# Attention with mixture-of-experts on one core: small vector work and clearing DMAs spread over the tiles of a row, and the last row's routing cut six to two

## The chip, the cores and the metric

The kernel runs on one core of a Trainium2 chip. The metric is the device time of one execution in microseconds (us), the median of three runs. The engines are named as in the profile: PE (TensorE, matrix products), DVE (VectorE), ACT (ScalarE), POOL (GpSimd) and SP (SyncE, which here only issues DMAs).

## What is computed

The input x has 8 rows of 1024 tokens with 128 features. The reference is, cut to what matters:

```python
x = x + attention(layernorm(x))       # 16 heads of 8, query l sees keys l-63 to l
x = x + moe(layernorm(x))             # 8192 tokens

# attention: softmax(q k / sqrt(8) over the 64 keys of the window) v, then Wo
# moe:
scores = softmax(xf @ w_router)       # 8 experts
expert_weights, top_experts = top_k(scores, 2)
order = argsort(flat_e, stable=True)  # tokens of an expert in order
slot = where(offsets < 2048, expert * 2048 + offsets, none)
xb = zeros(8 * 2048 + 1, 128).at[slot].set(xf[src])   # gather tokens by expert
h = gelu(xb @ w1); y = h @ w2         # per expert, 128 -> 512 -> 128
out = zeros(T, 128).at[src].add(weight * y) + bias
```

The slot of a token needs the count of all tokens ahead of it that chose the same expert, so routing goes through the rows in order.

## The kernel before

**Two phases.** Phase one does the attention, the router and the filling of `xb`, the buffer of tokens by expert in the chip's large memory. Phase two runs the experts over `xb`. The change touches phase one alone.

**Tiles.** Phase one is a loop over 64 tiles of 128 queries, 8 tiles for each of the 8 rows (L1163 to L1209; tile j of row b is called (b, j) below). Each turn of the loop does, in this order:

- `scores` of the tile two ahead: 32 small products per unit on PE (L557), then DVE takes the maximum over the keys (`mx`, L565) and prepares it in three 16-bit parts (L573). PE transposes `mx` (L582) and ACT copies it to `mxt` (L584).
- `attend` of the tile one behind: probabilities times values (`av`, L647), copied by ACT to `sums` (L655).
- if a group of tiles is complete, a `Context`: SP DMAs move the softmax denominators (`den`, L676) and the weighted values (`ctx`, L678) from `sums` into the feature layout. A group of four goes by another way, with one reciprocal on DVE (L688) between two rounds of DMAs (L673, L683, L690, L694). Later DVE divides (`scale`, L704 and L705).
- `probs` of the tile itself: the scores again in the transposed layout with the maximum taken off (`t`, L602, L619, L626), and ACT's exp (L632). The score buffers in PSUM are three, shared by `scores` and `probs`.

**Planned steps.** Between these go steps of the neighbouring rows, from a list `plan` written by hand. `at(b, j, ...)` puts a step to tile (b, j). In tile i the steps up to the second one that uses PE are issued at once, the rest (`behind`) in the next tile after `scores`. `pairs` holds ACT work that follows the context (exp of the router at L823, the `apply` of the second norm at L415), and `late` the division steps. The steps are:

- `first(b, ...)`: the attention's norm of row b. `stats` (DVE), `root` (an inverse square root by three Newton steps, L384 to L396, 13 instructions on DVE, more if part of it is on GpSimd), `rooted` (L403, L421), and `apply` (L410) for four tiles at a time, on DVE. `FOUR[0]` and `FOUR[1]` are the two halves of a row.
- `turn`, `queries`, `keys`, `values`, `spread`: the transposes and projections of the next row. `spread` sends `qt` and `kt` in block form to `qbd` and `kbd` by eight SP DMAs (L496, L499). `values` ends with two SP DMAs (L485, L487).
- `of(b, 0, ...)`: the routing of the row before. `out` (L781 to L787) is the output projection and residual, then `stats`, `root`, `softmax`, `choose` (top two, L831 to L849), `count` (PE, L858), `place` (running count, L870 to L879), `slots` (slot numbers, L887 to L890) and `keep` (adds the bias, L809, and stores the residual, L810).

`slots` also appends one scatter per token tile and choice to a queue; `put` (L903) takes them from it, as indirect DMAs issued by GpSimd, two per tile and three from row 5 on.

**Order on the engines.** The orders on PE, DVE, ACT and GpSimd are as written by hand. SP's is left to the scheduler. All engines work in order.

**Clears.** `clears()` zeroes `xb` by 16 SP DMAs of 528 KB (L315), each from a small zero tile `zeros` of four rows that is read over and over. The loop asks for one a tile from tile 1 (two from tile 14), but nothing makes the DMA wait, and the scheduler issues them all between 19 and 50 us.

**The last rows.** Row 6's routing is cut in two halves of four tiles, so that it can run inside row 7. Row 7's is done by `piece`: two pieces of four tiles, advanced by `go(piece, n)`, which does the next n of its steps. Some of these stand in the plan, the rest behind the loop, where no tiles hide them. There `put` sends out what is queued, and GpSimd sets a mark (`memset`, L1229) behind which PE does `stay_awake(38)`: 76 products of no use (L169), which keep PE's clock up until `xb` is complete.

Of the kernel before, what the change touches and what calls it, by code (L numbers as in the profile page):

```python
# [10 lines left out]
F32 = mybir.dt.float32  # L11
# [8 lines left out]
P = 128  # L20
# [4 lines left out]
E = 8  # L25
TOP_K = 2
FFN = 512
W = D + 4
# [14 lines left out]
def bc_mid(ap, n):  # L43

    return ap.unsqueeze(1).to_broadcast([ap.shape[0], n, ap.shape[1]])
# [3 lines left out]
def kernel(  # L49
# [13 lines left out]
    nc = tc.nc  # L63
    B, L, _ = x.shape
    NJ = L // P
# [4 lines left out]
    NS = CAP // P  # L70
# [21 lines left out]
    def after(ins, of):  # L92

        tc.add_manual_dep(
            ins, of.name,
            mybir.DependencyInfo(mybir.DependencyClass.Sync, mybir.DependencyReason.DATA),
            reason="a transfer in step with the tiles",
        )
# [17 lines left out]
    with ExitStack() as ph:  # L116
        c1 = ph.enter_context(tc.tile_pool(name="c1", bufs=1))
# [34 lines left out]
        for r in range(4):  # L152
            nc.sync.dma_start(
                out=wo_sb[r::4, 0:D],
                in_=wo.rearrange("(g r d) c -> r g d c", g=NQ, r=4)[r],
            )
        nc.sync.dma_start(
            out=bias_sb, in_=bias.rearrange("a b d -> (a b) d").to_broadcast([P, D])
# [33 lines left out]
        for t in (mt_32, mtf_32):  # L192
# [9 lines left out]
            out=i32s, in_=ident.rearrange("p (g q) -> p q g", g=4), axis=AX.X, op=ALU.add  # L202
# [45 lines left out]
        def permute():  # L248
# [15 lines left out]
        rev = c1.tile([P, E], F32, tag="rev", name="rev")  # L264
        limit = c1.tile([P, E], F32, tag="limit", name="limit")
        tok = c1.tile([P, NT], F32, tag="tok", name="tok")
        zeros = c1.tile([P, 4, W], F32, tag="zeros", name="zeros")

        go_on = {
            n: c1.tile([P, E * n], F32, tag=f"goon{n}", name=f"go_on{n}") for n in (2, 4, 8)  # L270
        }
        taken = [c1.tile([P, E], F32, tag=f"taken{i}", name=f"taken{i}") for i in range(2)]

# [36 lines left out]
        def clears():  # L310

            half = CAP // 2
            for i in range(2 * E):
                to = xb[i * half : (i + 1) * half, :].rearrange("(p n) d -> p (n d)", p=P)
                nc.sync.dma_start(  # L315
                    out=to.rearrange("p (m k) -> p m k", m=NS // 8),
                    in_=bc_mid(zeros.rearrange("p n d -> p (n d)"), NS // 8),
                )
                yield


        kt_b, kbd_b, qbd_b, xnt_b, mx_b = [], [], [], [], []
# [337 lines left out]
        class Context:  # L660
# [46 lines left out]
            def steps(self):  # L707

                if self.few:
                    return ((1, self.invert), (3, self.scale))  # L710
                return (
                    (1 + t * (self.b < 6), partial(self.scale, t)) for t in range(self.n)
                )

        def attend_last(b, j, pr):
# [203 lines left out]
        def at(b, j, call, *args):  # L919
            plan[b * NJ + j].append((call, args))  # L920
# [38 lines left out]
        at(0, 4, turn, 1, 1)  # L959
        at(0, 4, first, 2, "stats")  # L960
        at(0, 4, queries, 1, 1)
        at(0, 5, keys, 1, 1)
        at(0, 5, first, 2, "root", nc.gpsimd)
        at(0, 5, values, 1, 0)
        at(0, 7, first, 2, "rooted")
        at(0, 7, first, 2, "apply", FOUR[0])
        at(0, 7, values, 1, 1)
        at(1, 0, first, 2, "apply", FOUR[1])

        for b in range(1, B):
            f = (b - 1, 0)
            if b < 7:
                at(b, 0, of, *f, "out", 0, 3)
                at(b, 0, of, *f, "out", 3, 1)
                plan[b * NJ].insert(0, (begin, (b - 1, 0, NJ)))
            at(b, 1, values, b, 2)
            if b + 1 < B:
                at(b, 1, turn, b + 1, 0)  # L980
                at(b, 2, queries, b + 1, 0)
                at(b, 3, keys, b + 1, 0)
                at(b, 3, spread, b + 1, 0)
            if b < 7:
                at(b, 2, of, *f, "stats", range(2))
                at(b, 2, of, *f, "out", 4, 2)
                at(b, 3, of, *f, "out", 6, 2)
            if b + 1 < B:
                at(b, 4, values, b + 1, 0)
                at(b, 4, turn, b + 1, 1)  # L990
                at(b, 5, queries, b + 1, 1)
                at(b, 6, keys, b + 1, 1)
                at(b, 7, values, b + 1, 1)
            if b == 7:
                continue
            if b + 2 < B:
                at(b, 1, first, b + 2, "stats")
                at(b, 6, first, b + 2, "root", nc.vector)
                at(b, 7, first, b + 2, "rooted")
                at(b, 7, first, b + 2, "apply", FOUR[0])  # L1000
                at(b + 1, 0, first, b + 2, "apply", FOUR[1])
            at(b, 3, of, *f, "stats", range(2, 4))
            at(b, 3, of, *f, "root", nc.vector)
            n = b * NJ + 4
            for t, what, *args in (
                (n, "rooted"), (n, "softmax"),
                (n + 1, "choose", 0),
                (n + 2, "choose", 1),
                (n + 4, "slots"),
                (n + 4, "keep", (0,)), (n + 5, "keep", (2,)),  # L1010
                (n + 6, "keep", (4,)), (n + 7, "keep", (6,)),
            ):
                plan[t].append((of, (*f, what, *args)))
            pairs[n].append(partial(of, *f, "exp"))
            for i in range(4):
                pairs[n + i].append(partial(of, *f, "apply", range(2 * i, 2 * i + 2)))
            plan[n + 3].insert(0, (of, (*f, "count")))
            plan[n + 3].append((of, (*f, "place")))


        def half(b, j0, *steps):
# [32 lines left out]
        def piece(j0, j1):  # L1054
            f = (B - 1, j0)
            n = range(j1 - j0)
            calls = (
                (begin, B - 1, j0, j1, True),
                *((of, *f, "out", i, min(2, len(n) - i)) for i in range(0, len(n), 2)),
                (of, *f, "stats"),  # L1060
                (of, *f, "root", nc.vector),
                (of, *f, "rooted"),
                (of, *f, "softmax"),
                (of, *f, "exp"),
                (of, *f, "choose", 0),
                (of, *f, "apply", n),
                (of, *f, "choose", 1),
                (of, *f, "count"),
                (of, *f, "place"),
                (of, *f, "slots"),  # L1070
                (of, *f, "keep"),
            )
            return iter(calls)
# [3 lines left out]
                done = call(*args)  # L1077
            return done

        ends = [piece(0, 4), piece(4, 8)]  # L1080
        at(7, 4, go, ends[0], 2)
        at(7, 6, go, ends[0], 3)
        at(7, 7, go, ends[0], 5)
        at(7, 7, go, ends[1], 2)

        def values_end():
            for w in range(2):
# [69 lines left out]
        tiles = [(b, j) for b in range(B) for j in range(NJ)]  # L1157
        scores(0, 1)
        mxt = turn_max(0, 0)
        clearing = clears()  # L1160
        todo, late, behind, after_context = None, defaultdict(list), [], []
        for i, (b, j) in enumerate(tiles):
            if j == 0:  # L1163
                ctxs[b] = a2.tile([P, L], F32, tag="ctx", name=f"ctx_{b}")
                spread(b, 1) if b else None
            for _ in range(min(i, 1) if i < 14 else 2):
                next(clearing, None)
            ahead = tiles[i + 1] if i + 1 < len(tiles) else None


            def scores_ahead():
                if i + 2 < len(tiles):
                    put(1, scores(*tiles[i + 2]))

            if i:
                scores_ahead()
            for call, args in behind:
                call(*args)
            if todo is not None:
                begun, _ = attend(*todo)  # L1180
                put(1 if b >= 5 else 0, begun)
                if i - 1 in together:
                    context = Context(*together[i - 1])
                    for n, step in context.steps():
                        late[i + n if i < len(tiles) - 2 else i].append(step)
                for call in after_context:
                    call()
                after_context = []
            pr, mxt, done = probs(b, j, mxt, ahead)
            if not i:  # L1190

                for call, args in plan[0]:
                    call(*args)
                plan[0] = []
                scores_ahead()
            todo = (b, j, pr)
            put(1, done)
            if 2 <= j < 6:
                load_x(b + 3, slice(2 * j - 4, 2 * j - 2), done)
            if i in (34, 42):  # L1200
                ahead_w.append(load_w(len(ahead_w), done))

            n = [n for n, step in enumerate(plan[i]) if is_product(*step)][1:2]
            n = n[0] if n else len(plan[i])
            for call, args in plan[i][:n]:
                call(*args)
            behind = plan[i][n:]
            after_context = pairs[i]
            for call in late[i]:  # L1209
                call()  # L1210
# [3 lines left out]
        put(len(puts))  # L1214


        for which, n in ((0, 2), (1, 2), (0, 2)):
            go(ends[which], n)
        put(2)
        for n in (2, 1, 2):  # L1220
# [160 lines left out]
```

## Time and profile before

| What | Time |
|---|---|
| median of three runs | 761.75 us (760.16 to 764.14) |
| the profiled execution, device time | 762.97 us |
| span of its trace | 761.2 us |
| granted PE clock, mean | 0.941 of full speed |
| start to 47 us | PE busy 37.4 us, DVE 28.7, DMA engines 66% |
| row 2 to 3 (152 to 204 us) | PE busy 45.7 us, DVE 41.0, DMA engines 35% |
| row 7 (360 to 449 us with row 6's end) | PE busy 70.5 us, DVE 70.7, DMA engines 26% |
| between loop and experts (449 to 495 us) | PE busy 13.5 us, DVE 17.5, POOL 28.5, clock 0.58 |
| experts (495 to 761 us) | PE busy 242.4 us, DVE 35.4, POOL 197.5 |

The rows are parts of one profiled execution; the columns give the busy time in each stretch, which adds up work that overlaps. The device time of that execution is 1.8 us over its span, since what lies ahead of the first and behind the last instruction is not in the trace. The busy time of an engine says how much it has to do; which wait ends last in a stage has to be read from the order of the instructions there.

### The profile page before, as it was taken

The numbers are of one execution on the slowest core, as the hardware profiler recorded it, in microseconds if no ns is written. First come the engines' busy times: TensorE is split into PE (matmuls) and PEld (weight loads), VectorE is DVE, ScalarE is ACT, GpSimd is POOL, SyncE is SP. The second block draws the span as 40 slices with busy tenths as digits, with TensorE's granted clock in tenths as the row PEclk, the third lists the DMA queues.
The fourth block names the chain that finished last, engine by engine and source line by source line (L and its number), as shares of the span: only waits on it lengthen the run. The fifth ranks groups of instructions, "written<-read, shape, count | busy, mean of one in ns | idle before, by whom it ended". The sixth has DMA issues, their size and how long they took to land.

```text
span 761.2 us, 21771 instructions
## 1 busy us (share of the span) xinstructions
PE 634.9 (83%) x8777; PEld 468.5 (62%) x8777; DVE 389.3 (51%) x1219; ACT 364.3 (48%) x637; POOL 361.9 (48%) x366
## 2 busy tenths in 40 slices
PE   8789698897987987988979641599999999999990
PEld 7445455454555544554545430589999999898990
DVE  6664577978688778788887764121111111111010
ACT  5446367566565674674664520023444444443430
POOL 7001000332432434505416447438778787787876
PEclk9999899999999999999998965699999999999996
DMA  2982313333243433333322111236456365463333
GB/s 76 325 294 77 91 58 97 97 115 116 81 123 108 130 107 112 123 96 104 111 84 86 59 45 54 78 102 109 53 106 109 43 123 93 52 119 34 36 31 31
DMA packets 78308, 74.00 MB, mean 97 GB/s; under 512 B 13907, under 2 KB 63928, under 8 KB 77312
## 3 DMA queue, kind: packets, MB, share of 16 engines
q1 hardware_dynamic: 55296, 55.59, 23.2%
q0 software_dynamic: 22528, 16.74, 15.8%
q8 instruction: 69, 1.13, 0.7%
q14 instruction: 31, 0.25, 0.1%
q10 hardware_dynamic: 384, 0.28, 0.1%
HBM read 19.14 MB, written 30.28 MB: 65 GB/s over the span
## 4 chain that ended last, share of the span: by engine, by line
PE 28%; issue 17%; DVE 14%; POOL 14%; ACT 11%; DMA 9%; SPq 6%; POOLq 0%; DVEq 0%; ACTq 0%
POOL out_dram L1310 12%; ACT pr L632 7%; PE av L647 5%; PE t L619 5%; PE yp L1300 5%; PE hp L1289 4%; DMA out_dram<-ye,dest 4%; DVE mx L565 3%; SPq L676 2%; DMA ctx<-sums 2%; ACT mxt L584 2%; SPq L678 2%; PE t L602 2%; PE po L781 2%; PE t L626 1%
## 5 line engine op out<-in xcount | busy, mean ns | idle before, releaser
L903 POOL DMA_INDIRECT xb<-xn,si x128 | 125.5, 980 | 226.4 <-PE t L626 64.5
L1310 POOL DMA_INDIRECT out_dram<-ye,dest x128 | 197.5, 1543 | 68.4 <-issue 27.4
L632 ACT ACTIVATE pr<-t 128x1024 f32<-128x1024 f32 x128 | 123.9, 1019 | 55.0 <-PE t L626 46.2
L565 DVE TENSOR_REDUCE mx<-s 128x8 f32<-128x768 f32 x128 | 116.3, 951 | 41.0 <-PE s L557 40.9
L1300 PEld LDWEIGHTS yp<-w,hT 128*128 128x128 f32 x1024 | 124.7, 193 | 9.3 <-ACT hT L1293 6.3
L1300 PE MATMUL yp<-w,hT 128*128 128x128 f32 x1024 | 126.1, 276 | 4.6 <-DVE ye L1305 3.9
L1289 PE MATMUL hp<-xts,w 128*128 128x256 f32 (+1 forms) x528 | 122.4, 375 | 0.3 <-DVE xts L1280 0.3
L1293 ACT ACTIVATE hT<-hp 128x512 f32<-128x512 f32 x128 | 76.4, 597 | 70.3 <-PE hp L1289 68.3
L1305 DVE TENSOR_TENSOR ye<-yp,gt 128x256 f32<-128x256 f32 (+1 forms) x66 | 27.1, 415 | 161.7 <-PE yp L1300 138.9
L1289 PEld LDWEIGHTS hp<-xts,w 128*128 128x128 f32 x528 | 94.1, 192 | 10.2 <-DVE xts L1280 0.6
L655 ACT COPY sums<-av 128x512 f32<-128x512 f32 x63 | 36.9, 586 | 100.6 <-PE av L647 90.7
L647 PE MATMUL av<-pr,vbd 128*32 128x128 f32 x2016 | 71.1, 282 | 7.6 <-ACT vbd L480 2.7
L619 PE MATMUL t<-qbd,kt 32*128 32x256 f32 x1024 | 74.0, 391 | 0.4 <-issue 0.3
L647 PEld LDWEIGHTS av<-pr,vbd 128*32 128x32 f32 x2016 | 53.1, 112 | 28.9 <-ACT mxt L584 9.3
L557 PE MATMUL s<-kbd,qt 32*32 32x384 f32 x2048 | 61.0, 506 | 4.5 <-DMA kbd<-kt 4.5
L1280 ACT COPY xts<-xt 128x256 f32<-128x256 f32 (+1 forms) x57 | 21.0, 369 | 88.0 <-PE xt L1278 88.0
L619 PEld LDWEIGHTS t<-qbd,kt 32*128 32x128 f32 x1024 | 51.1, 192 | 4.4 <-issue 2.3
L809 POOL TENSOR_TENSOR x<-x,bias_sb 128x256 f32<-128x256 f32 x28 | 21.3, 764 | 51.7 <-ACT xn L415 51.4
L781 PE MATMUL po<-wo_sb,ctx 128*128 128x136 f32 x128 | 25.8, 327 | 19.9 <-DVE lg L787 9.0
L781 PEld LDWEIGHTS po<-wo_sb,ctx 128*128 128x128 f32 x128 | 18.9, 207 | 37.2 <-issue 14.9
L704 DVE RECIPROCAL den<-den 128x128 f32<-128x128 f32 x39 | 36.8, 944 | 7.5 <-DMA den<-sums 7.1
L602 PE MATMUL t<-i,mt 32*128 32x256 bf16 x448 | 28.6, 280 | 13.6 <-DVE mx L565 7.4
(185 smaller groups left out, 745.8 us busy)
## 6 DMA issues: line engine op xcount, KB each, us to landing
xb<-zeros SPq DMA_DIRECT2D x16, 528.0 KB
xe<-xb SPq DMA_DIRECT2D x7, 1056.0 KB
vbd<-vbd SPq DMA_DIRECT2D x32, 192.0 KB
kbd<-kt SPq DMA_DIRECT2D x62, 72.0 KB
qbd<-qt SPq DMA_DIRECT2D x64, 64.0 KB
out_dram<-x SPq DMA_DIRECT2D x32, 128.0 KB
w<-in_L_ffn_w_dram SPq DMA_DIRECT2D x16, 256.0 KB
x<-in_L_attn_x_dram SPq DMA_DIRECT2D x22, 128.0 KB
```

The source lines that it names most:

```text
L557: done = nc.tensor.matmul(place(g, slice(32 * blk, 32 * (blk + 1))), lhsT=qt[quad(g), q0 : q0 + 32], rhs=kbd[quad(g), :, c0 + 32 * blk : c ...
L565: nc.vector.tensor_reduce(out=part_of(mx, 0)[:, 2 * u : 2 * u + 2], in_=units[u][:, :, 0 : 4 * KB].rearrange("p g (r k) -> p g r k", r=4), ...
L602: nc.tensor.matmul(to, lhsT=mt[quad(g), 0, hq, :], rhs=i32[quad(g)].rearrange("p (w r) q -> p w r q", w=2), start=hq == 0, stop=False, ski ...
L619: nc.tensor.matmul(units[g // 2][:, g % 2, w], lhsT=kt[quad(g), q0 : q0 + P], rhs=qbd[quad(g), :, c0 : c0 + 64], start=False, stop=False, ...
L632: nc.scalar.activation(pr[:, 2 * u : 2 * u + 2], units[u], AF.Exp)
L647: last = nc.tensor.matmul(av[quad(g), k, :, w], lhsT=pair_values(vbd, 2 * j + w, g, k), rhs=pr[:, g, w, 2 * k : 2 * k + 2, :], start=True, ...
L781: nc.tensor.matmul(po[:, k, :], lhsT=ctxs[self.b][:, t0 : t0 + P], rhs=wo_sb, start=True, stop=True,)
L903: ins = nc.gpsimd.indirect_dma_start(out=xb[:, :], out_offset=bass.IndirectOffsetOnAxis(ap=slot, axis=0), in_=row, in_offset=None, bounds_ ...
L1289: nc.tensor.matmul(hp[:, c], lhsT=ws[e][0][:, (c0 + c) * P : (c0 + c + 1) * P], rhs=xt, start=True, stop=True,)
L1293: nc.scalar.activation(hT[:, c0 : c0 + per], hp, AF.Gelu_apprx_tanh)
L1300: nc.tensor.matmul(yp[:, k, :], lhsT=hT[:, c, k * P : (k + 1) * P], rhs=ws[e][1][:, c, :], start=c == 0, stop=c == NC - 1,)
L1310: add = nc.gpsimd.indirect_dma_start(out=acc, out_offset=bass.IndirectOffsetOnAxis(ap=dests[e][:, n : n + 1], axis=0), in_=ye[:, k, :], in ...
```

## The change

- **Clears.** `zeros` has two rows instead of four, so that a clear reads 264 floats (1056 bytes) at a time, and twice as many such chunks. `clears` is a generator that is sent the last product of `probs` of the preceding tile, and its DMA waits for it (`after`). One clear goes with each tile from tile 1, two with tile 14.
- **First norm.** `root` and `rooted` of row b+2 stand first in tile (b, 3)'s plan (formerly in tiles 6 and 7), `apply` for the two halves in tiles 5 and 6 (formerly tile 7 and tile 0 of the next row). For row 2 the root goes from GpSimd to DVE, with the like steps in row 0; `keys(1, 1)` comes a tile later there, behind `values(1, 0)`.
- **Routing of rows 0 to 4.** `slots` and the first `keep` come a tile later.
- **Routing of row 5** (done in row 6): `choose(1)`, `count` and `place` come a tile sooner, and `slots` at the end of tile (6, 7), a tile sooner than before.
- **Context steps.** In row 7 the division steps of a group are spread over tiles as in rows 0 to 5; only in row 6 they stay together.
- **Last row.** The pieces are six and two tiles instead of four and four, with other `go` steps: two at tile 5, nine at tile 7, and three instead of two in the second turn behind the loop. `go_on`, a constant by piece width, gets the width 6.

```diff
-        zeros = c1.tile([P, 4, W], F32, tag="zeros", name="zeros")
+        zeros = c1.tile([P, 2, W], F32, tag="zeros", name="zeros")
...
-            n: c1.tile([P, E * n], F32, tag=f"goon{n}", name=f"go_on{n}") for n in (2, 4, 8)
+            n: c1.tile([P, E * n], F32, tag=f"goon{n}", name=f"go_on{n}") for n in (2, 6, 4, 8)
...
+            behind = yield
             for i in range(2 * E):
                 to = xb[i * half : (i + 1) * half, :].rearrange("(p n) d -> p (n d)", p=P)
-                nc.sync.dma_start(
-                    out=to.rearrange("p (m k) -> p m k", m=NS // 8),
-                    in_=bc_mid(zeros.rearrange("p n d -> p (n d)"), NS // 8),
-                )
-                yield
+                into = nc.sync.dma_start(
+                    out=to.rearrange("p (m k) -> p m k", m=NS // 4),
+                    in_=bc_mid(zeros.rearrange("p n d -> p (n d)"), NS // 4),
+                )
+                after(into.ins, behind.ins)
+                behind = yield
...
-                    (1 + t * (self.b < 6), partial(self.scale, t)) for t in range(self.n)
+                    (1 + t * (self.b != 6), partial(self.scale, t)) for t in range(self.n)
...
-        at(0, 5, keys, 1, 1)
-        at(0, 5, first, 2, "root", nc.gpsimd)
         at(0, 5, values, 1, 0)
-        at(0, 7, first, 2, "rooted")
-        at(0, 7, first, 2, "apply", FOUR[0])
+        at(0, 5, first, 2, "root", nc.vector)
+        at(0, 5, first, 2, "rooted")
+        at(0, 6, keys, 1, 1)
+        at(0, 6, first, 2, "apply", FOUR[0])
+        at(0, 6, first, 2, "apply", FOUR[1])
         at(0, 7, values, 1, 1)
-        at(1, 0, first, 2, "apply", FOUR[1])
...
-                at(b, 6, first, b + 2, "root", nc.vector)
-                at(b, 7, first, b + 2, "rooted")
-                at(b, 7, first, b + 2, "apply", FOUR[0])
-                at(b + 1, 0, first, b + 2, "apply", FOUR[1])
+                plan[b * NJ + 3].insert(0, (first, (b + 2, "root", nc.vector)))
+                plan[b * NJ + 3].insert(1, (first, (b + 2, "rooted")))
+                at(b, 5, first, b + 2, "apply", FOUR[0])
+                at(b, 6, first, b + 2, "apply", FOUR[1])
...
-            n = b * NJ + 4
+
+            n, soon = b * NJ + 4, b == 6
...
-                (n + 2, "choose", 1),
-                (n + 4, "slots"),
-                (n + 4, "keep", (0,)), (n + 5, "keep", (2,)),
+                (n + 2 - soon, "choose", 1),
+                (n + 5 - 2 * soon, "slots"),
+                (n + 5, "keep", (0,)), (n + 5, "keep", (2,)),
...
-            plan[n + 3].insert(0, (of, (*f, "count")))
-            plan[n + 3].append((of, (*f, "place")))
+            plan[n + 3 - soon].insert(0, (of, (*f, "count")))
+            plan[n + 3 - soon].append((of, (*f, "place")))
+            if soon:
+                step = (of, (*f, "slots"))
+                plan[n + 3].remove(step)
+                plan[n + 3].append(step)
...
-        ends = [piece(0, 4), piece(4, 8)]
-        at(7, 4, go, ends[0], 2)
-        at(7, 6, go, ends[0], 3)
-        at(7, 7, go, ends[0], 5)
-        at(7, 7, go, ends[1], 2)
+        ends = [piece(0, 6), piece(6, 8)]
+        at(7, 5, go, ends[0], 2)
+        at(7, 7, go, ends[0], 9)
...
-        clearing = clears()
+        clearing, done = clears(), None
+        next(clearing)
+        cleared = 0
...
-                next(clearing, None)
+                if cleared < 2 * E:
+                    clearing.send(done)
+                    cleared += 1
...
-        for which, n in ((0, 2), (1, 2), (0, 2)):
+        for which, n in ((0, 2), (1, 3), (0, 2)):
             go(ends[which], n)
```

## The prediction

> **What bounds the kernel now.** The page first: TensorE is busy 83% of the span, and after 495 us it is busy in nearly every slice; that last part, the expert layer, is not touched. So the change can only act before 495 us.
>
> ```profile
> span 761.2 us, 21771 instructions
> ...
> PE 634.9 (83%) x8777; PEld 468.5 (62%) x8777; DVE 389.3 (51%) x1219; ACT 364.3 (48%) x637; POOL 361.9 (48%) x366
> ...
> PE 28%; issue 17%; DVE 14%; POOL 14%; ACT 11%; DMA 9%; SPq 6%; POOLq 0%; DVEq 0%; ACTq 0%
> ```
>
> DVE is on the chain for 14%, SP's queue with the DMAs it issues for 15%. The stage table then gives 52 us for each of rows 1 to 6 (8 tiles), DVE 40 to 43 us of them. Starts of the softmax's exp (L632) in the timeline lie 5.7 us apart in a quiet tile, 6.4 to 6.8 in tiles 5 and 0, and 8.1 to 9.8 from tile 1 to tile 2 of rows 2 to 6. That long one I followed in the chain of waits and the timeline, here between rows 4 and 5: first SP's queue, then what DVE does at its end. Columns are start, duration, then what ran, in brackets the idle time before it and what ended that.
>
> ```profile
> 275.77 2.29 SPq L694 DMA_DIRECT2D den<-one_4518i  x4
> 278.16 2.96 SPq L676 DMA_DIRECT2D den<-sums  x4
> 281.16 2.50 SPq L678 DMA_DIRECT2D ctx<-sums  x4
> 283.76 2.45 SPq L499 DMA_DIRECT2D kbd<-kt  x4
> 286.31 3.53 SPq L496 DMA_DIRECT2D qbd<-qt  x4
> 289.94 0.67 SPq L485 DMA_DIRECT2D vbd<-vbd  x1
> 290.65 0.65 SPq L487 DMA_DIRECT2D vbd<-vbd  x1
> 291.42 2.56 SPq L676 DMA_DIRECT2D den<-sums  x4
> 294.02 3.58 SPq L678 DMA_DIRECT2D ctx<-sums  x4
> ```
>
> ```profile
> 298.93 0.68 DVE L705 TENSOR_TENSOR ctx<-ctx,den 128x128 f32<-128x128 f32 x1 [0.89 <-DMA ctx<-sums]
> ...
> 299.85 1.82 DVE L565 TENSOR_REDUCE mx<-s 128x8 f32<-128x768 f32 x2 [0.24 <-PE s L557]
> ```
>
> Two things end here together. DVE has 9 us of small work between the maxima (L565) of two tiles. And SP issues 30 DMAs, 0.6 to 0.9 us each, with hardly a pause from 275.77 to 297.60, the last of which (plus 1.3 us to land) DVE waits for in front of the next tile's maximum. The slack between the two is small: DVE waits for ctx at that place in each row, by 0.5 to 2.2 us.
>
> At the start SP sits in six clears while TensorE wants keys that are queued behind them:
>
> ```profile
> 24.29 7.25 SPq L315 DMA_DIRECT2D xb<-zeros  x6
> ...
> 38.36 0.49 SPq L499 DMA_DIRECT2D kbd<-kt  x1
> 40.29 1.44 PE L557 MATMUL s<-kbd,qt 32*32 32x384 f32 x32 [3.37 <-DMA kbd<-kt]
> 41.66 1.94 PE L647 MATMUL av<-pr,vbd 128*32 128x128 f32 x32
> ```
>
> **Part 1, clears.** 16 DMAs of 528 KB stay 16; each now waits for the preceding tile's last probability product, so one is issued per tile (two at tile 14). Six issues took 7.25 us; with one there instead of six, kbd lands 3 to 5 us sooner and the 3.37 us stall goes. The clock row: in the 4 us behind that stall the granted clock was 0.5, and av took 1.94 us instead of its usual 1.08. The Trainium skill's "TensorE: Matmul & The Clock Gate", "Why this matters for your kernels", says not to leave TensorE idle for more than about 3 us, as the clock then halves; the trace agrees at 3.37. By the wait alone the gain is 3.37, and 0.3 for the issue gap behind it; with the products that ran halved on the path +0.35 more: -4.0 (3.6 to 5).
>
> What speaks against it: a chunk falls from 2112 to 1056 bytes, 512 chunks a clear instead of 256. "DMA: Bandwidth & Descriptors", "Bandwidth", wants transfers batched to a MiB or more. Nearest row: packets of 2112 B took 93 ns each in this trace, of 1024 B 58, so a clear holds the 16 engines 1.9 us (512 x 60 ns / 16) instead of 1.5: 6 us more for all 16, in time when the engines are 29 to 40% busy: hidden, at 0; if it isn't, +0.4 for each clear that a waited-for landing meets.
>
> SP's turn is not hidden. Rows 0 and 1 have the same tight run of small DMAs, formerly free of clears. An issue of a clear takes 0.65 (1.29 for two at 48.43) to 1.21 us (six in 7.25[...]); I take 0.65. Row 0 to 1: `keys(1, 1)` comes a tile later, which takes four kbd issues (3.3 us) from ahead of the first ctx landing; two clears (1.3) take their place, so the maximum behind it is 2.0 sooner. The kbd issues then stand ahead of the second landing, and 0.8 is left: -0.8 (-1.5 to +1.2). Row 1 to 2: five clears and one output DMA ("keep") in the chain, 5 x 0.65 + 0.5 less about 1.2 that a wait for a landing hides: +2.6 (+1.5 to +5).
>
> **Part 2, VectorE's work.** Summing DVE's instructions between two maxima, tile 1 to tile 0 in a steady row: before 6.1, 4.2, 8.4, 3.8, 5.5, 2.7, 5.8, 5.8 us; after 4.8, 4.2, 5.5, 4.5, 5.5, 5.3, 5.8, 6.8. The sum, 42.3, is unchanged: the normalization's root (13 instructions, 2.3 us) and two groups of four applies (1.1 each) only move. Tile 3 loses 3.0 us, so DVE no longer sets the 9 us there. But the next maximum stands behind L705, which waits for the ctx landing, and SP's 30 issues are untouched. So only the slack comes back: from the waits of ctx and the maxima's starts in each row, -1.75 (rows 2 to 3), -1.8 (3 to 4), -0.65 (4 to 5), 0 (5 to 6). Against it, the four applies put at tile 5 stand ahead of the reciprocal L688 (271.52), whose result SP's chain waits for: 1.03 us more, of which about half hides in DVE's wait for the softmax pair's exp (0.32 here) and the gap behind it: +0.56 in rows 4 to 5 and 5 to 6; in the two earlier rows L688 itself waited 1.1 to 1.3 us for its DMA, at nothing. One "keep" more in row 5 to 6's chain: +0.45. Together -1.75 -1.8 -0.1 +1.0 = -2.65. Row 2's root goes from GpSimd to DVE (ten instructions, 2.3 us) in row 0, where DVE waits 5 us for scores: at nothing (0 to +2).
>
> **Part 3, slots.** One tile later for rows 0 to 4: 0.72 us of DVE moved to a tile with room; the scatters (L903) of a row start at its end anyhow. Row 5's come a tile sooner than before, which moves two scatters of 1.28 us out of the queue behind the loop, where GpSimd waits 4.96 us for the last slots anyway: 0.
>
> **Part 4, row 7.** Row 5's `count`, a step on PE, leaves tile (6, 7)'s plan, so the second PE step there comes later and more is issued at once: by the written order place, slots and the whole root of row 6's first half now fall between the maxima of (7, 1) and (7, 2). DVE's work ahead of the maxima of (7, 0) to (7, 7) becomes 9.2, 2.7, 10.1, 4.9, 6.2, 4.5, 7.0, 6.1 (before 7.8, 4.1, 5.8, 9.3, 6.2, 4.5, 8.1, 5.5). The periods were 8.1, 5.1, 6.0, 9.4 in the first four; I get 9.5, 5.0, 10.2, 7.65 (a wait of DVE for ACT's exp at L823 stands behind an exp pair of 1.94 us): +3.7; the last four -0.9, as the two-tile piece's additions leave tiles 6 and 7. Sum +2.8 (+1 to +5): this row has little SP work, so here DVE's sum is the period.
>
> **Part 5, the end.**
>
> ```profile
> 480.62 1.09 POOL L903 DMA_INDIRECT xb<-xn,si  x1 [4.96 <-issue]
> ...
> 484.25 0.14 POOL L1229 MEMSET nothing<- 128x1 f32 x1
> 484.44 10.12 PEld L169 LDWEIGHTS awake<-ident 128*128 128x128 f32 x76 [8.90 <-issue]
> 484.44 10.31 PE L169 MATMUL awake<-ident 128*128 128x128 f32 x76 [8.76 <-issue]
> ...
> 495.19 0.41 PE L1278 MATMUL xt<-ident,xe 128*128 128x128 f32 x2 [0.44 <-DMA xe<-xb]
> ```
>
> Only 4 scatters follow the last slots instead of 8: 4 x 1.28 = 5.1 us. But 76 filler products (10.31 us) start at the memset's mark, still behind the third scatter, and TensorE does the filler before the first expert. Scatters that end sooner are hidden behind it. The DVE chain ahead of the slots grows by 0.7 us (four more additions, three statistics). 0.2 of it hides: +0.5 (-1.7 if the DVE gaps of about 1 us at 465 to 479 shrink, to +0.7).
>
> **Sum.** -4.0 - 0.8 + 2.6 (clears and start) - 2.65 (rows 2 to 6) + 2.8 (row 7) + 0.5 (end) = -1.55. The profiled execution took 762.97 (span 761.2 and 1.8 around it), 1.2 above the median; from the median 761.75 - 1.55 = 760.2.
>
> **Rivals.** A, the SP chain is not the pin: TensorE, DVE and SP give way together, tile 1 to 2 shrinks from 9 to about 6 in five rows, 5 x 3 = 15 instead of 2.65: 760.2 - 12.4 = 747.8, and half of it, if the chain moves up with what it waits for, 754. For: its start hangs on L688 and qbd waits for TensorE, so some of it moves with them. Against: the unbroken issue. B, the clears hold SP's queue: seven of them stand in the run of small DMAs of rows 0 to 2. At 1.21 us (the row of six in a run) 7 x 0.56 = 3.9 more, and where a ctx landing falls behind a clear's 512 chunks, 1.9 at each of two boundaries: 760.2 + 7.7 = 767.9. It makes the kernel slower by over 3.8 us when a clear costs 0.87 us of issue with both landings delayed, or 1.4 without.[...] C, the start gains nothing because another wait (ACT's work for the same keys) follows at once: 764, within 0.5%.
>
> **Chances.** 0.34 for the forecast, 0.28 for A with its half, 0.24 for B, 0.14 for C. The forecast's own spread (757 to 764) leaves a little on each side. A change of 0.5% (3.8 us) is about what a measurement of this kernel can tell from none; by this, faster 0.34, same 0.36, slower 0.30. Range: A's half and B are in it, A whole is left out: 750 to 768.5.
>
> **What would show it.** In the profile after: no wait for kbd at 40 us and clock near 1 there; tile 1 to 2 at 8 to 9.5 us in rows 4 to 6 with DVE's L705 waiting 2 to 4 us for ctx (if the tile is 6 us, A); clears' issues at 0.65 or over 1 us between rows 1 and 2 (B); row 7's third period near 10 us; filler still ending within 1 us of the first expert product. What would make me wrong is above all that SP's run is elastic, or that row 7's bunched work is covered.

## The result and the profile after

The changed kernel takes 770.61 us (median of six, 767.83 to 777.9) against 762.41 us before (six runs): a ratio of 1.0104, 95% interval 1.0069 to 1.0139. It is slower by 8 us where I forecast 1.5 faster; 770.6 is also over the range's 768.5.

The kernel before stands at 762 to 763 us in two sets of runs (this one among them) and at 752 to 754 in four, so every ratio below is against runs of the kernel before in the same set.

Three lines of the page after: the span is 4.5 us longer. On the chain that ended last DVE has 21% instead of 14 and SP's queue 10% instead of 6; this is the loop, where the chain runs less over PE and ACT than before. PE's 38% instead of 28 and GpSimd's 7% instead of 14 are of the experts, where it now runs over PE's products and less over GpSimd's scatters of the result (L1310, 12% before), though the experts take the same time to about 2 us.

```profile
span 765.7 us, 21780 instructions
...
PE 642.0 (84%) x8777; PEld 472.6 (62%) x8777; DVE 393.7 (51%) x1229; ACT 364.2 (48%) x637; POOL 358.9 (47%) x355
...
PE 38%; DVE 21%; issue 10%; SPq 10%; ACT 8%; POOL 7%; DMA 7%; POOLq 0%; DVEq 0%; ACTq 0%
```

From the starts of exp (L632 before, L634 after) in the two timelines I made a ledger. It says by how much a stretch is longer after than before, in us (where a tile's time is given below, it runs from the start of the exp of the tile ahead to its own). The third column is the same from a second profile of each kernel, taken in one set ("before, again" and "after, again" below):

| Stretch | Measured | Again | Forecast |
|---|---|---|---|
| up to exp of (0,0) | -1.0 | -0.6 | 0 |
| (0,0) to (1,1): the start | -4.0 | -5.7 | -4.0 |
| (1,1) to (1,4): row 0 to 1 | +4.8 | +4.6 | -0.8 |
| (1,4) to (2,5): row 1 to 2 | +7.7 | +5.8 | +2.6 |
| (2,5) to (6,5): rows 2 to 6 | -6.5 | +1.9 | -2.65 |
| (6,5) to (7,7): row 7 | +4.6 | +4.5 | +2.8 |
| (7,7) to the first expert product | +1.0 | -1.5 | +0.5 |
| experts, to the span's end | -2.1 | -0.6 | 0 |

The sums are +4.5 and +8.4. The device times of the first pair differ by 4.9 (762.97 and 767.83); the other 3.3 us of the medians' 8.2 lie between these two executions and their medians, for the profiled execution of the changed kernel is the fastest of its six. Rows 2 to 6 are the stretch that differs most from profile to profile. At the start the forecast held: one clear stands ahead of the keys, and the products follow without a stall and at full clock (av 1.08 us instead of 1.94).

```profile
34.63 0.56 SPq L316 DMA_DIRECT2D xb<-zeros  x1
...
35.83 0.94 PE L559 MATMUL s<-kbd,qt 32*32 32x384 f32 x32
...
37.01 1.08 PE L649 MATMUL av<-pr,vbd 128*32 128x128 f32 x32 [0.24 <-ACT mxt L586]
```

Between rows 1 and 2 SP's queue of the changed kernel reads so:

```profile
120.13 0.62 SPq L316 DMA_DIRECT2D xb<-zeros  x1
120.84 0.60 SPq L812 DMA_DIRECT2D out_dram<-x  x1
121.55 1.07 SPq L692 DMA_DIRECT2D one_1767i<-one  x1
...
123.27 0.56 SPq L316 DMA_DIRECT2D xb<-zeros  x1
126.30 2.32 SPq L696 DMA_DIRECT2D den<-one_1767i  x4
```

A clear's issue takes only 0.56 to 0.62 us, less than my 0.65. What takes long is the trip of the small reciprocal (L692) through memory: its readers are issued 4.75 us behind its own issue, where before it was 2.3:

```profile
120.01 0.44 SPq L690 DMA_DIRECT2D one_1750i<-one  x1
...
122.32 2.30 SPq L694 DMA_DIRECT2D den<-one_1750i  x4
```

At this place the trip took 4.7 to 5.0 us in all seven traces with a waiting clear a tile on SP's queue (this one and six of the runs below), and 1.6 to 2.4 in twelve without. DVE then waits 5.5 us in one piece for the denominators that they bring; in that stretch of before there is no such wait.

### The profile page after: what moved, and what is told of

The parts are those of the page before. It is cut to its first block, busy times and chain, and to the rows that moved or that the text cites. A ratio compares the mean times of both kernels' runs of the same rounds, so it can differ in the third digit from the quotient of the medians.

```text
span 765.7 us, 21780 instructions
## 1 busy us (share of the span) xinstructions
PE 642.0 (84%) x8777; PEld 472.6 (62%) x8777; DVE 393.7 (51%) x1229; ACT 364.2 (48%) x637; POOL 358.9 (47%) x355
## 3 DMA queue, kind: packets, MB, share of 16 engines
q8 instruction: 69, 1.13, 0.7%
## 4 chain that ended last, share of the span: by engine, by line
PE 38%; DVE 21%; issue 10%; SPq 10%; ACT 8%; POOL 7%; DMA 7%; POOLq 0%; DVEq 0%; ACTq 0%
PE yp L1309 12%; PE hp L1298 12%; DVE mx L567 6%; ACT pr L634 5%; POOL out_dram L1319 4%; PE t L621 3%; SPq L678 3%; PE av L649 3%; SPq L680 3%; DMA ctx<-sums 2%; DVE den L706 2%; PE xt L1287 1%; ACT mxt L586 1%; DMA out_dram<-ye,dest 1%; PE s L559 1%
## 5 line engine op out<-in xcount | busy, mean ns | idle before, releaser
L634 ACT ACTIVATE pr<-t 128x1024 f32<-128x1024 f32 x128 | 123.9, 1019 | 75.3 <-PE t L628 69.7
L1302 ACT ACTIVATE hT<-hp 128x512 f32<-128x512 f32 x128 | 76.4, 597 | 70.4 <-PE hp L1298 66.9
L1298 PEld LDWEIGHTS hp<-xts,w 128*128 128x128 f32 x528 | 93.3, 190 | 10.2 <-DVE xts L1289 0.6
L621 PE MATMUL t<-qbd,kt 32*128 32x256 f32 x1024 | 78.2, 404 | 0.0
L621 PEld LDWEIGHTS t<-qbd,kt 32*128 32x128 f32 x1024 | 54.3, 196 | 2.4 <-issue 1.2
L604 PE MATMUL t<-i,mt 32*128 32x256 bf16 x448 | 31.7, 279 | 19.9 <-DVE mx L567 18.5
L586 ACT COPY mxt<-pm 128x512 bf16<-128x512 bf16 x64 | 37.7, 589 | 1.5 <-PE pm L584 1.5
L543 PE MATMUL s<-ms,i 32*128 32x256 bf16 x256 | 28.7, 281 | 10.0 <-ACT pr L634 6.3
```

The lines of the kernel that those rows point to most:

```text
L586: nc.scalar.copy(mxt.rearrange("p r w q -> p (r w q)"), pm.rearrange("p r q -> p (r q)"))
L621: nc.tensor.matmul(units[g // 2][:, g % 2, w], lhsT=kt[quad(g), q0 : q0 + P], rhs=qbd[quad(g), :, c0 : c0 + 64], start=False, stop=False, ...
L634: nc.scalar.activation(pr[:, 2 * u : 2 * u + 2], units[u], AF.Exp)
L1298: nc.tensor.matmul(hp[:, c], lhsT=ws[e][0][:, (c0 + c) * P : (c0 + c + 1) * P], rhs=xt, start=True, stop=True,)
L1302: nc.scalar.activation(hT[:, c0 : c0 + per], hp, AF.Gelu_apprx_tanh)
```

## Experiments

Three theories stood after this. **1**: the clears hold SP's queue and the landings of rows 0 to 2, and the moved norm is good. **2**: rows 0 to 2 lose by the moved norm steps. **3**, later: the end and the slots, which I had put at nothing, carry the loss. "Norm alone" below is the kernel before with the first norm's edits (and row 0's, `keys(1, 1)` among them).

**The clears in four forms, and the norm alone.** First the changed kernel without the waits on the clears:

```diff
-                after(into.ins, behind.ins)
-                behind = yield
+                yield
```

> The changed kernel, but its clears wait for nothing, as before (chunks of 1056 bytes kept). Theory 1, the clears' 528 KB stand ahead of the small DMAs of rows 0 to 2 and delay their landings: the 12.6 us lost between (1,1) and (2,5) come back, less the start's gain of 5: 770.6 - 7.6 = 763. Theory 2, the loss of rows 0 to 2 comes from the moved norm steps and keys(1,1): only the start's gain goes, 770.6 + 5 = 775.6.

Measured: ratio 1.0149 (1.0115 to 1.0184). The loss of (1,1) to (2,5) went down from 12.6 to 1.9 us and the start's gain went, as theory 1 says for these stretches; but the total is still 1.5% over before, so a larger loss is elsewhere. In the kernel before, only the clears' edits:

> The kernel before with the new clears alone. Theory 1: start -5, rows 0 to 2 about +12: 762.4 + 7 = 769.5. Theory 2: the start's gain stays, 757.5.

Measured: 1.0036 (1.0018 to 1.0054), 756.28 against 752.83. They cost 3.5 us: less than theory 1 wanted, and no gain, against theory 2. Only the norm's edits:

> The kernel before with the moved first norm (and keys(1,1) a tile later) alone. Theory 1: the trace's rows 2 to 6 gave 6.5 us, so 762.4 - 6.5 = 756. Theory 2: rows 0 to 2 lose some 8 with it, about 764. My forecast's step alone was -2.65, 759.8.

Measured: 0.9864 (0.9837 to 0.9891), 743.01 us against 752.83. This part gains 9.8 us, more than theory 1 hoped, and theory 2 is out. A second set:

> The kernel before with the moved first norm alone, once more, as the measure for this call. Some 1.4% under the kernel before, as in its first call, or 2% where the kernel before has the gaps at its end and this one does not.

Measured: 0.9872 (0.9846 to 0.9898), 742.66. Then the changed kernel with `nc.gpsimd.dma_start` for the clears:

> The changed kernel with the clears issued by GpSimd instead of SP, same waits and bytes. Theory 1 in its narrow form (a small DMA waits because it is behind a clear in SP's own queue): most of the 12.6 us come back and the start's gain stays, 758 to 761. If the bytes themselves are in the way, whichever queue they come from: 767 to 771.

Measured: 1.0164 (1.0133 to 1.0195), 766.71 us, about what I gave for the bytes. From (1,1) to (2,5) 3 to 5 of the 10 to 13 us came back, not most of them. With the clears off SP's queue the reciprocal's trip is short (1.7 us), but DVE waits 3.44 us for `one<-total` in row 1 (in the same stretch of the kernel before there is no such wait):

```profile
120.78 0.55 DVE L690 RECIPROCAL one<-one 128x64 f32<-128x64 f32 x1 [3.44 <-DMA one<-total]
```

So a landing on SP's queue comes late beside clears of another queue. The Trainium skill, "DMA: Bandwidth & Descriptors", "Queues, rings and completion order", has the rule for it: a DMA's completion lands only after every earlier write of that DMA engine, across its queues. The run agrees with it, but can't tell it from a plain sharing of the DMA engines' time. Next, the early clears again, and one 4 KB store a tile with the wait of the changed kernel:

```diff
+                if tinies < 2 * E:
+                    into = nc.sync.dma_start(out=tiny[:, tinies], in_=zeros[:, 0, 0:8])
+                    after(into.ins, done.ins)
+                    tinies += 1
```

> The changed kernel with the clears not waiting (as in the earlier run), and besides one 4 KB store a tile to a scratch buffer, with the wait of the changed kernel's clears: the issues and waits without the bytes. If issue and wait on SP's queue are the price, rows 0 to 2 (start of exp of (1,1) to (2,5)) are some 10 us longer than with early clears, as in the changed kernel; if the 528 KB are, 1 to 2 us longer.

Measured: a single run, 773.25 us. From (1,1) to (1,4) it is 4.6 us longer than with early clears alone, about what the changed kernel loses there; from (1,4) to (2,5) only 1.1. But the 1.1 is held down by (2,2), which is long with early clears (9.0 us against 7.3). The tile where the clears act is (2,0): it takes 6.7 us with early clears, 9.9 with the 4 KB stores and 12.7 in the changed kernel. So in row 0 to 1 the issues and waits in SP's order are the price, in row 1 to 2 they are about half of it and the bytes the other half. This rests on one trace. Last, the norm alone with waiting clears in places that looked quiet:

```diff
-            for _ in range(min(i, 1) if i < 14 else 2):
+            for _ in range({1: 2, 2: 3, 3: 4, 4: 4, 11: 3}.get(i, 0)):
```

> The moved norm with waiting clears (chunks of 2112 bytes), but put where no small landing is waited for: 2, 3, 4 and 4 in tiles 1 to 4 of row 0 and 3 in tile 3 of row 1. If the clears cost by the place, the start's 4.6 us are kept and rows 0 to 2 lose nothing: 4 to 5 us under the run with the moved norm alone. If waiting clears cost anywhere, it is level with it or over it.

Measured: 742.55 us against the norm alone's 742.66. Tile (0,2) became 4.7 us shorter and (0,6) 7.3 us longer: the start's stall was only pushed on.

**The end and rows 5 to 7.** Before, again:

> The kernel before once more, for a profile beside the others of this call. In its first profile VectorE had gaps of about 1 us between instructions at 465 to 479 us, some 7 us in all, which no later profile of a related kernel has. If they belong to the kernel, they are here again and the last scatter ends about 49 us behind the last exp pair's start; if they were of that execution, the scatters run without a break and it is about 42 us.

The gaps are there again. Here are two of them in VectorE's rows (in brackets the idle time):

```profile
465.01 0.19 DVE L836 TENSOR_REDUCE xn<-lg 128x4 f32<-128x32 f32 x1 [1.21 <-DVE lg L833]
...
467.81 0.19 DVE L841 TENSOR_REDUCE xn<-rk 128x4 f32<-128x32 f32 x1 [1.21 <-DVE rk L839]
```

The same two instructions in the norm alone, which has the same code there:

```profile
456.98 0.19 DVE L836 TENSOR_REDUCE xn<-lg 128x4 f32<-128x32 f32 x1
...
457.66 0.19 DVE L841 TENSOR_REDUCE xn<-rk 128x4 f32<-128x32 f32 x1
```

From the last exp pair to the last scatter's end the kernel before takes 49.2 us, the norm alone 42.3 and 44.5, in sets in which the kernel before took some 10 us less. What makes the gaps stays open. After, again, in the set of before, again:

> The changed kernel once more, as the measure for the kernels of this call. Between 1.0% (as on record) and 2% over the kernel before: 2% if the gaps of VectorE in the first profile of before were not of the kernel, as then its end is 7 us shorter than the profile showed and the change's loss at the end 8 us instead of 1.

Measured: 1.0055 (1.0031 to 1.0078), under what I expected. Then the changed kernel with `soon`, the `!= 6` and the pieces undone:

> The changed kernel with the routing of row 5, row 7's context steps and the two pieces of four as before; clears and norm changed. Theory 1, the end: the filler's mark stands one scatter ahead of the last instead of five, which costs 5 us, and rows 6 to 7 lose 3 to 5 by bunched steps: 8 to 12 us below the changed kernel of the same call. Theory 2, the loss lies in the clears: within 3 us of it.

Measured: 1.0093 (1.0055 to 1.0130). Row 6's tiles 6 and 7 got back 3.4 of 3.7 us, but the gaps came back with the old pieces, and the last scatter ended 53.8 us behind the last exp. By the total (770.65 us against 767.37 for the changed kernel in that set) neither theory held. The changed kernel with one line left out, so that the mark comes ahead of the last four scatters:

```diff
-        put(3)
```

> The changed kernel with the filler's mark ahead of the last four scatters instead of the last one; nothing else moves. If the filler is what the first expert waits for, 3 x 1.28 = 3.8 us less; if the scatters are, nothing.

Measured: 1.0005 (0.9977 to 1.0033), 763.65 against 767.37 us for the changed kernel in that set: -3.7, as worked out. In the traces the time from the last exp pair to the first expert product falls from 52.1 to 48.3 us. And `soon` set to `False`:

> The changed kernel with row 5's routing as for the other rows (choose, count and place a tile later, slots two). If count's leaving tile (6, 7) bunches row 6's steps, the 5 us from tile (6, 5) to (6, 7) go; two scatters more come at the end, 2.6 us. About 2 to 3 us under the changed kernel.

Measured: 1.0171 (1.0127 to 1.0214), 767.86 us. The changed kernel was not run in this set, so the total can't be set against it; from (6,5) to (6,7) the 5 us are gone, as expected. The scatters left for the end are six more, not two: 33 begin behind the start of the last exp pair, against 27 in the changed kernel.

**Slots.** The norm alone with `slots` and the first `keep` at n + 5, then each by itself:

```diff
-                (n + 4, "slots"),
-                (n + 4, "keep", (0,)), (n + 5, "keep", (2,)),
+                (n + 5, "slots"),
+                (n + 5, "keep", (0,)), (n + 5, "keep", (2,)),
```

> The moved norm alone, with slots and the first keep a tile later for all rows, as the change has it for rows 0 to 4. The changed kernel's rows 2 to 6 came out 2 to 6 us longer than with the moved norm alone, in single tiles of up to 10 us. If the later slots are the cause, this one is 3 to 6 us slower than the norm alone; if not, it is level in rows 2 to 5 and some 2 us slower at the end (two more scatters behind the loop).

Measured: 1.0015 (0.9989 to 1.0042), 752.46: 9.8 us over the norm alone.

> The moved norm with slots alone a tile later (keep stays). If slots on VectorE or the scatters' queue, which fills a tile later, is the cause, most of the 9.8 us of both together: 1.0 to 1.3% over the norm alone, about level with the kernel before. If keep is, level with the norm alone (1.3% under before) but for 1 to 2 us at the end.

Measured: 1.0013 (0.9988 to 1.0037), 754.65: 11.6 us over the run with keep alone, which follows and is of the same set.

> The moved norm with the first keep alone a tile later. In tile (b, 2)'s stall of the run with both, GpSimd did two bias additions (1.43 us) in a row ahead of a scatter, the scatter came 1 us later and beside the ctx DMAs, and these took 2.7 instead of 1.4 us to land. If that is the cause, this run has the loss (5 to 8 us over the norm alone, tile 1 to 2 of some rows about 10 us); if slots is, it is level with the norm alone.

Measured: 0.9867 (0.9831 to 0.9904), 743.08, level with the norm alone. It is slots, not keep, against my reading. The changed kernel with both back at n + 4:

> The changed kernel with slots and the first keep of rows 0 to 4 where they were (and row 5's slots in the tile they have in the changed kernel). If the later slots cost the same beside the other parts, 7 to 10 us under the changed kernel: level with the kernel before or a little faster, -0.5% to +0.6% by the chip. If the other losses cover it, +1%.

Measured: 1.0110 (1.0073 to 1.0147), 760.71 us, so without the later slots the rest of the change still loses 1.1%. In its set the kernel with row 5's routing undone, which has the later slots, takes 7.2 us more; the changed kernel itself was not there.

Where do the late slots cost? One part is at the end: with the later slots 33 scatters begin behind the start of the last exp pair, with the norm alone 30. These three, 3.8 us at 1.28 each, are of row 5, whose slots these two kernels move later too. The changed kernel moves row 5's sooner and has 27, with the later slots of rows 0 to 4 and without.

The other part is in tiles 1 and 2 of rows 2 to 6: together they take 71.0 and 70.4 us with later slots, 66.9 and 63.8 in the two traces of the norm alone and 67.4 with keep alone. Here is (4,2) with both later, and below it the same tile with the norm alone:

```profile
237.79 2.51 SPq L678 DMA_DIRECT2D ctx<-sums  x4
...
243.06 0.29 DVE L705 TENSOR_TENSOR ctx<-ctx,den 128x128 f32<-128x128 f32 x1 [2.91 <-DMA ctx<-sums]
...
244.27 0.61 PE L602 MATMUL t<-i,mt 32*128 32x256 bf16 x6 [3.18 <-DVE mx L565]
...
244.47 2.12 PE L619 MATMUL t<-qbd,kt 32*128 32x256 f32 x16
```

```profile
236.14 2.51 SPq L678 DMA_DIRECT2D ctx<-sums  x4
...
240.02 0.29 DVE L705 TENSOR_TENSOR ctx<-ctx,den 128x128 f32<-128x128 f32 x1 [1.51 <-DMA ctx<-sums]
...
241.24 0.39 PE L602 MATMUL t<-i,mt 32*128 32x256 bf16 x6 [0.99 <-DVE mx L565]
...
241.37 1.13 PE L619 MATMUL t<-qbd,kt 32*128 32x256 f32 x16
```

The issues take the same 2.51 us, but the landing is 2.8 us behind them instead of 1.4. TensorE idles 3.18 us instead of 0.99, and its next products take 2.12 instead of 1.13 us: the granted clock is 0.5 from 244 to 247 us, as the clock rule has it that I cited for the start. Its 3 us are no sharp bound here: in (5,2) of this trace a wait of 2.13 us was followed by a clock of 0.5 (the products took 1.89 us), in (6,2) one of 2.77 us was not (1.13 us). The tile is 10.2 us long instead of 6.8.

The late landing is not most of it: (5,2) and (6,2) take 8.8 and 8.6 us in this trace with a landing of 1.4. Over the five boundaries from row 1 to row 6 the two traces with later slots are longer than the three without by 1.8 us (means) from the maximum of tile 4 to the reciprocal's issue, by 1.2 until SP issues its readers, by 1.6 in SP's run that follows, and by 0.1 from there to the next maximum of tile 4. VectorE's own work is not what holds the maximum up, since in all these tiles DVE waits for ctx ahead of it (1.5 to 2.9 us in this trace).

Over all traces a late landing (2.4 to 3.3 us) that DVE waited for in rows 3 and 4 went with a scatter begun 0.6 to 1.6 us ahead of the last issue's end. Not each such scatter made a late landing. I held that scatter back, in both kernels:

```diff
+            held = int(j == 2)
-                    put(1, scores(*tiles[i + 2]))
+                    put(1 - held, scores(*tiles[i + 2]))
-                put(1 if b >= 5 else 0, begun)
+                put(1 - held if b >= 5 else 0, begun)
-            put(1, done)
+            put((3 if b >= 5 else 2) if held else 1, done)
```

> The moved norm and later slots, with the scatter in tile 2 of each row held back until that tile's probabilities are done. If a scatter beside the ctx DMAs is what makes the landing late, no tile 2 of rows 3 to 6 is over 8 us and the ctx landing is 1.3 to 1.5 us: 4 to 6 us of the 11 come back, about 748, 0.7% under the kernel before. If the later slots cost by another way, it stays level with the kernel before.

Measured: 0.9996 (0.9978 to 1.0014), 751.63. Tiles 2 of rows 3 to 5 were 6.0 to 7.3 us, but rows 2 and 6 had 9.7 and 10.1, row 2 with a landing of 2.9 us and row 6 with one of 1.4, and no scatter near either.

> The moved norm alone with the same scatter held back. Its ctx landings were mostly in time already, so little is to be had: level with the norm alone or up to 2 us under it, 741 to 743, 1.3 to 1.6% under the kernel before.

Measured: 0.9903 (0.9873 to 0.9933), 744.70: nothing gained. The scatter is not shown to be the cause. What makes these landings late, and what else makes the tiles long, stays open.

## Why the prediction was wrong

Two steps failed wholly, each a cost that I put at nothing or nearly so: the slots (part 3) and what the clears do to rows 0 to 2 (part 1). The norm was mis-sized, and the end is right only by its number.

**Part 3, slots: the step that failed is "the scatters (L903) of a row start at its end anyhow".** I costed the 0.72 us of DVE and took it that nothing else moves. But the scatters come a tile later with the slots: in row 6 the two tiles without any are (6,6) and (6,7) with the norm alone, (6,7) and (7,0) with later slots. Measured beside the norm alone, or keep alone in the other set, the later slots cost 9.8 to 11.6 us. Of that the 3.8 us at the end belong to row 5, and the changed kernel does not have them; some 6 to 8 us are left by the medians, 3 to 7 by tiles 1 and 2 in the traces. What in the later scatters makes these tiles longer stays open. A smaller slip of mine is that row 5's slots take three scatters out of the queue behind the loop, not two (27 left instead of 30).

**Part 2, the norm: right in its mechanism, too small.** SP's run is untouched, to 1 us, as I said. For rows 2 to 6 of the first profile of before and of the norm's second run I cut the time from the reciprocal to the maximum of tile 4 into the trip of the reciprocal (L690's issue to L694's), SP's run to the last ctx issue, and the rest to the maximum:

| Boundary | trip before, norm | run before, norm | rest before, norm |
|---|---|---|---|
| 2 to 3 | 2.8, 1.8 | 21.0, 20.8 | 3.3, 1.5 |
| 3 to 4 | 2.7, 1.5 | 21.0, 22.0 | 3.4, 1.6 |
| 4 to 5 | 3.7, 1.9 | 21.8, 21.4 | 2.3, 1.5 |
| 5 to 6 | 2.5, 3.2 | 21.2, 21.7 | 3.3, 1.7 |

The rest shrank by 1.8, 1.9, 0.7 and 1.6: three of my four slacks to 0.1 us; the fourth, which I had put at 0, was another 1.6. That closeness is in part luck: from the second profile of before to the first of the norm the rest shrank by only 0.8, 0, 0.1 and 1.1. What I had not in the sum at all is the trip, -1.0, -1.2, -1.8 and +0.7 us (-0.6, -0.4, -1.9 and +0.6 in the other pair). Its place between rows 4 and 5 in the norm's queue, which is to be read against the first fence of the prediction:

```profile
264.55 0.34 SPq L690 DMA_DIRECT2D one_4532i<-one  x1
...
266.42 2.29 SPq L694 DMA_DIRECT2D den<-one_4532i  x4
...
285.29 2.50 SPq L678 DMA_DIRECT2D ctx<-sums  x4
```

Why the trip is shorter was not tried. The reciprocal came 1.1 us later between rows 4 and 5 (forecast 0.56) and not at all later between 5 and 6. Row 0 gained 2 to 4 us more, by which profile of before it is set against, where I had given the root's move nothing and `keys(1, 1)` went into the clears' sum. In size this part did more than rival A's half: some 10 us. One of my signs also pointed to A: the long period, which by exp is that of tile 1 (I wrote tile 1 to 2), is 5.3 to 5.7 us in rows 4 to 6 of the changed kernel and not 8 to 9.5, with L707 waiting 1.5 to 1.6 us for ctx and not 2 to 4. But SP's run did not give way, as A has it, and part of the time is now in tile 2 (6.5 to 8.5 us instead of 5.6 to 6.1) and, in rows 4 and 5, in tile 5.

**Part 1, the clears: the start right, the rest mis-sized.** The stall at the start went (tile (0,2) takes 5.1 us instead of 9.8), and -4.0 for its stretch held. The exact number is luck: in the same stretch the norm alone saves 3 us at (1,0) (10.4 us instead of 13.6), which the changed kernel does not keep (13.5). Row 0 to 1 failed: +2.0 to +4.8 in the six traces of the change's clears on SP's queue, instead of -0.8. The issues and waits alone make 4.6 there, and the clears alone nothing, so this loss is of clears beside the moved norm. Between rows 1 and 2 it is +7.7 and +5.8, and +4.5 with the clears alone, against +2.6.

My figure of 0.65 for an issue was right, and the halved chunks cost nothing: their packets took 47 ns in the mean, where I had estimated 60, so a clear holds the DMA engines 1.5 us (512 x 47 ns / 16) as before. The terms that I left at zero are the wait for a product that each clear brings into SP's order, and its bytes ahead of a waited-for landing. Rival B had the second (1.9 at two boundaries); its other, the issue of 1.21 us, hardly occurred: the issues are 0.55 to 0.62 us but for one of 1.36 us.

**Part 4, row 7: right.** I forecast 10.2 us between the maxima of (7,1) and (7,2); the trace has 395.76 - 385.57 = 10.19, with row 5's place in it:

```profile
385.57 1.82 DVE L567 TENSOR_REDUCE mx<-s 128x8 f32<-128x768 f32 x2 [3.48 <-PE s L559]
...
387.76 0.28 DVE L872 TENSOR_TENSOR_SCAN upto<-go_on,pc 128x64 f32<-128x64 f32 x1
...
395.76 1.81 DVE L567 TENSOR_REDUCE mx<-s 128x8 f32<-128x768 f32 x2
```

Of the neighbours, (7,0) was 9.6 (9.5) and (7,3) 7.7 (7.65). (7,1) was 6.2 instead of 5.0, and the last four together 0.8 us shorter (forecast 0.9). Undoing row 5's routing took the early part of the loss away. Sum +4.6 for +2.8, inside its bounds.

**Part 5, the end: +0.5 came out as +1.0 and -1.5, by luck; the row I read was not one to lean on.** I let the DVE chain set the end and the mark fall behind the third last scatter at the same time as before. In the changed kernel the scatters run almost without a break and set the end, and the mark is one scatter ahead of the last instead of five:

```profile
490.10 0.14 POOL L1238 MEMSET nothing<- 128x1 f32 x1
...
490.29 11.70 PE L169 MATMUL awake<-ident 128*128 128x128 f32 x76 [14.30 <-POOL nothing L1238]
490.43 0.97 POOL L905 DMA_INDIRECT xb<-xn,si  x1 [0.19 <-issue]
...
501.83 0.38 PE L1287 MATMUL xt<-ident,xe 128*128 128x128 f32 x2
```

So the filler, which I called a cover, is itself what the first expert waits for. Moving the mark by three scatters gave 3.7 us back; for the four by which it moved, 4 x 1.28 = 5.1 us is an estimate. In both profiles of before this hides behind the gaps at its end: without these before's end is 4.7 to 6.9 us shorter, as in the norm alone, and the change loses that much more. That fits the kernels with most of the change, which stand 1.1 to 1.7% over before in the sets where before takes 752 to 754; the change itself was not run in one.

So the norm, some -10 us for my -2.65, is more than eaten up by terms that I had at nothing or too small: the slots (an estimated +6 to +8 for 0, from the medians less the scatters of row 5), the clears (+4.7 to +8.5 in the ledger's three stretches from (0,0) to (2,5), for -2.2), row 7 (+4.6 for +2.8) and the mark (+3.7 to +5.1 for +0.5). They act on each other, and I don't claim that they add up to the microsecond. The best kernel here is the norm alone, 1.3% under before.

## What to carry to other kernels

When a step is moved, follow what it feeds (here a queue of scatters and the DMAs beside them), not only its own time on its engine. A DMA on the path has a price beyond its issue: what it waits for in its queue's order, the bytes written ahead of another landing, and the clock if TensorE then idles for two to three us. Test the parts of a composite change alone: here one part was worth 1.3%, and the others ate it.

## What was not expected of the hardware

With clears issued by GpSimd VectorE still waited 3.4 us for a small transfer of SP's queue. Gaps of 0.51 and 1.21 us between small dependent VectorE instructions, beside scatters that run without a break, came in each of three profiles with the pieces of four from the two sets in which before takes 762 to 763 us, and in none from the other sets. The changed kernel, with its pieces of six and two, had none in the same two sets. A trip of 32 KB through memory and back took 1.5 to 3.7 us at the same place of the program.
